# L0's tail: six row additions and six squeeze products on GpSimd, and a new order of the tail's steps

## The chip, the cores and the metric

The kernel runs on one core of one Trainium2 chip. The metric is the time of one execution in microseconds (us). A core has five engines that run their own instruction queues in program order and wait for each other through semaphores: TensorE (PE, matmuls; its weight loads are listed as PEld), VectorE (DVE), ScalarE (ACT), GpSimd (POOL) and SyncE (SP, which here issues most of the DMAs). All data is float32.

## The reference

The reference sends x, 8 batches of 512 tokens with 128 features (32 tiles of 128 tokens), through four layers, L0 to L3. Each layer is half a feed-forward part, an attention part, and half a feed-forward part again:

```
x = x + 0.5 * ffn(LN(x));  x = x + attention(LN(x));  x = x + 0.5 * ffn(LN(x))
```

L0's feed-forward part is a mixture of experts: a router takes the two best of eight experts for each token, with a capacity of 512 rows for each expert. Seven experts are two matrix products with a ReLU between them (128 to 512 to 128), the eighth hands the token through. L1's feed-forward part picks for each token one of 64 small splines by the scores of a cluster and of a tile, compresses the token to two numbers (a product to 32 features, Gelu, a second product to 2 numbers, tanh), evaluates the spline on them, adds the result along a learned direction and normalises again. L1's attention has 16 heads with rotary positions. L2 and L3 follow with other feed-forward and attention parts; the change has nothing to do with them except that some of their weights are made ready inside L0.

## The kernel before

x stays in SBUF for the whole kernel, as one tile of 128 partitions by 4 x 128 elements for each batch. L0 (`l0_block`, lines 493 to 915) runs in stages: the first norms and routing (an order written out by hand in the string FIRST), the first round of experts, MIDDLE (returned rows, attention, second routing), the second round of experts, and then the tail.

**A round of experts** is `experts(wk, ps, n, beside)`. POOL fetches each expert's 512 rows by four indirect DMAs (`fetch`, L664), PE turns them (`turn`, gp L676), PE makes the hidden rows (`inner`, hp L684, with ReLUs on ACT and DVE) and the results (`outer`, op L694), ACT scales them (y L697), and POOL scatters them by four indirect DMAs (`put`, L668) into a DRAM array `yds[n]`. Line order is program order: after each expert's puts a share of the list `beside` is issued. In the first round this list holds `zeros(1)` (four 1 MB DMAs on SP's queue which fill `yds[1]` with zeros from a tile `z`), the handed-through part (`self_part`) of the eight batches, and L1's weights. In the second round it holds the eight `self_part`s, the eight products of L3's adapter weights (`multiply`: pp L1912 on PE, wall L1913 on ACT, then a load of a later pair) and nine steps that add up L2's chosen weights (`adds`). Seven of the eight products are so issued ahead of the last expert's outer product, two of them behind the second expert, and the eighth follows behind the last expert. The round of experts has the PSUM tiles gp/op (tag mm), hp and pp, two buffers for each of the first two tags.

**The tail** is `l0_tail` (lines 919 to 968), called from `l1_block`. Here every engine's order is fixed by the string TAIL, which names steps; for a batch b they are:

- `load` b: two DMAs of 256 KB on SP's queue bring the two sets of returned rows (r, L482); `both` b adds them (L485); `add` b adds the sum to x (L488). For b above 1, `both` is on POOL; `add` is on POOL only if `returned` was called with `aside`, which MIDDLE does and the tail does not.
- `d_sums`, `d_scale`, `d_turn`, `d_keep`: the layer norm of a batch. The first pair of batches is measured on DVE (L248 to L263), the later pairs on POOL (L215 on DVE, L219 to L234 on POOL).
- `squeeze` b in three steps, from `l1_ffn_front`: `_0` the scores (sp L1048, copy L1049), `_1` the first product's bias and Gelu (ht L1054, L1055), `_2` the second product: the multiplication cm (L1060), the reduction cp (L1061) and tanh (comp L1063).
- `ffn0` and `ffn1`: fifteen steps of the spline part (`l1_ffn_steps`, L1087 to L1176) for the batches 0 and 1, with `update0`; `enter` is the norm of L1's attention for batch 0.
- `project0`, `project1`: the projections to q and k with rotary positions (pp L1242, rt L1248, rs L1251); `spread` m g: a permutation by matmuls and its copy (L1263, L1265, L1267); `values`: L1272.
- `turns`: two loads of tables (1 MB and 256 KB); `clear`: memsets on POOL (L1218).

In the order before, `project0` stands in the middle of the string, and the last line is `values ffn1_13 squeeze6_1 clear11 ffn1_14 squeeze7_2 spread02 spread03 spread00 squeeze6_2 spread01`. After the tail L1's attention starts with the scores of batch 0 (s L1290) and the row maxima (nm L1291).

Of the kernel before, what the change touches and what calls it, by code (L numbers as in the profile page):

```python
# [8 lines left out]
F32 = mybir.dt.float32  # L9
I32 = mybir.dt.int32  # L10
AF = mybir.ActivationFunctionType
ALU = mybir.AluOpType
# [46 lines left out]
shares4 c_scale7 whole6 stored7 table7 enter6 shares6 enter7  # L59
"""  # L60
TAIL = """
load1 both1 load0 add1 both0 add0 load3 load6 d_sums0 d_scale0 both3 d_turn0 both6 load2 add3 add6
d_keep0 load4 d_scale1 squeeze0_0 load7 both2 both4 d_turn1 ffn0_0 add2 d_sums2 squeeze0_1 load5 ffn0_1
d_scale3 d_keep1 ffn0_2 d_scale2 turns ffn0_3 add4 ffn0_4 d_turn3 both5 ffn0_5 ffn0_6 both7 d_turn2 add5
squeeze0_2 d_sums4 d_keep2 ffn0_7 squeeze1_0 ffn0_8 squeeze2_0 ffn0_9 d_keep3 ffn1_0 add7 ffn0_10
d_scale4 ffn1_1 ffn1_2 ffn0_11 d_sums6 d_scale5 squeeze2_1 ffn0_12 squeeze1_1 ffn0_13 ffn0_14 ffn1_3
d_scale6 d_turn6 d_scale7 squeeze1_2 d_turn4 d_keep4 d_turn5 squeeze3_0 d_turn7 update0 d_keep5 d_keep6
enter_0 ffn1_4 squeeze4_0 enter_1 squeeze3_1 d_keep7 squeeze5_0 ffn1_5 ffn1_6 clear10 squeeze2_2
squeeze3_2 squeeze5_1 project1 ffn1_7 ffn1_8 spread13 spread12 squeeze4_1 ffn1_9 squeeze5_2 ffn1_10
spread11 spread10 squeeze7_0 clear12 squeeze4_2 project0 ffn1_11 squeeze6_0 ffn1_12 clear02 squeeze7_1  # L70
values ffn1_13 squeeze6_1 clear11 ffn1_14 squeeze7_2 spread02 spread03 spread00 squeeze6_2 spread01
"""

L1F_PLACES = (-63, -58, -58, -55, -50, -50, -48, -47, -42, -42, -39, -37, -34, -31, -26, -22)
# [70 lines left out]
class Net:  # L145
# [316 lines left out]
        return w  # L462

    def zeros(self, n):
        for k in range(4):
            self.nc.sync.dma_start(
                out=self.yds[n][2048 * k : 2048 * k + 2048, :].rearrange("(p n) d -> p (n d)", p=P), in_=self.z)
# [24 lines left out]
    def l0_block(self, w):  # L492
# [8 lines left out]
        with ExitStack() as c:  # L501
# [154 lines left out]
            def experts(wk, ps, n, beside):  # L656
# [23 lines left out]
                def inner(e):  # L680
                    h = hs[e] = wk.tile([P, 4, 512], F32, tag="h", name="h")
                    for ic in range(4):
                        hp = ps.tile([P, 512], F32, tag="hp", name="hp")
                        nc.tensor.matmul(hp, lhsT=w["w1"][:, e, ic * P : (ic + 1) * P], rhs=gts[e], start=True, stop=True)  # L684
                        if ic % 2:
                            nc.vector.tensor_scalar(h[:, ic, :], hp, 0.0, None, ALU.max)
                        else:
                            nc.scalar.activation(h[:, ic, :], hp, AF.Relu)
# [197 lines left out]
                slots(bank)  # L886
            with tc.tile_pool(name="f0w", bufs=2) as wk, tc.tile_pool(name="f0e", bufs=2, space=PSUM) as ps, ordered(engines={*FIXED, mybir.EngineType.SP}):
                more = [lambda: box.__setitem__("w1", self.l1_ffn_weights(self.keep))]
                experts(wk, ps, 0, [lambda: self.zeros(1)] + [lambda b=b: self_part(b) for b in range(NB)] + more)
            with tc.tile_pool(name="f0m", bufs=2) as wk, tc.tile_pool(name="f0c", bufs=7, space=PSUM) as ps, ordered(engines=every):  # L890
                todo, bank = {}, banks(ps)
                load, both, add = self.returned(wk, self.yds[0], 3, True)
# [14 lines left out]
            with tc.tile_pool(name="f0w", bufs=2) as wk, tc.tile_pool(name="f0e", bufs=2, space=PSUM) as ps, ordered(engines=FIXED):  # L907
                w2, more = box["w2"]
                w3, steps = self.l3_ffn_weights(self.keep, wk, ps)
                parts = [lambda b=b: self_part(b) for b in range(NB)]  # L910
                experts(wk, ps, 1, [work for works in zip(parts, steps, more(ps)) for work in works] + [more(ps)[8]])
        return box["w1"], w2, w3

    def apart(self, group, ins):
# [4 lines left out]
    def l0_tail(self, w1, wk, bank, room, clear, turns, enter):  # L919

        todo = {}
        load, both, add = self.returned(wk, self.yds[1], 4)

        def at(name, n, work, *args):
            todo[name] = n, lambda: work(*args)
# [10 lines left out]
        for g in range(4):  # L936
            n = 9 * g
            for k in range(2):
                b = 2 * g + k
                at(f"load{b}", n - 30, load, b)  # L940
                at(f"both{b}", n + 1.3 * k, both, b)
                at(f"add{b}", n + 1.5 + 1.3 * k, add, b)
                scores, *others = self.l1_ffn_front(b, w1, bank, lambda name, shape, k=k: wk.tile([P, *shape], F32, tag=f"{name}{k}", name=name))
                chain(f"squeeze{b}", (n + (16 if b else 14.5) + 1.5 * k, n + 16 + 1.5 * k, n + 19 + 1.5 * k), lambda _, b=b, scores=scores: scores(self.xt[b]), *others)
            self.norms(todo, "d", (2 * g, 2 * g + 1), n + 3.5, bank, quick=not g)
        at("turns", -20, turns)
# [91 lines left out]
    def kept(self, xt):  # L1038
        return xt[:, 0:288].rearrange("p (i c) -> p i c", c=72)

    def l1_ffn_front(self, b, w, bank, room):

        nc = self.nc

# [12 lines left out]

        def finish(ht):
            cm, cp = room("cm", (4, 2, 32)), room("cp", (4, 2))
            nc.vector.tensor_tensor(cm, bc(ht, 2, 2), bc(w["cw2"].rearrange("p (n j) -> p n j", n=2), 1, 4), ALU.mult)  # L1060
            nc.vector.tensor_reduce(cp, cm, AX.X, ALU.add)  # L1061
            for n in range(2):
                nc.scalar.activation(w["comp"][b][:, :, n], cp[:, :, n], AF.Tanh, bias=w["cb2"][:, n : n + 1])  # L1063
# [1026 lines left out]
```

## Time and profile before

| What | us |
| --- | --- |
| Three timed runs | 2604.12, 2608.65, 2613.46 |
| Their median | 2608.65 |
| The profiled execution | 2601.68 |
| Its span in the profile | 2599.8 |
| First experts, fetch to last put (in the span's time) | 59 to 131 |
| Second experts | 259 to 337 |
| Tail, from the first POOL work after the puts to the first s of L1 | 336.6 to 417.0 |

The mean granted TensorE clock of the profiled execution is 0.963. Over the whole span PE is busy 91% of the time, DVE 78%, ACT 68%, POOL 44%. Times in the views are in us from the span's start. A timeline row gives start and duration, engine, line, operation, output and inputs, shapes and, in brackets, the engine's idle time before it with what ended it; the count at the end says how many instructions lie in the row. A window row gives for each engine the busy time in that stretch and the number of instructions, then the granted clock (PEclk), the DMA share and the transfer rate.

### The profile page before, as it was taken

The page shows a single profiled execution, that of the slowest core. Times are in us where ns is not written, and L with a number is a line of the kernel's source. Part 1 is how long each engine was busy: PE and PEld are TensorE (multiplying, and loading weights), DVE is VectorE, ACT ScalarE, POOL GpSimd, SP SyncE. Part 2 cuts the span into 40 slices and gives each one's busy share as a digit, 9 for nine tenths or more (in the row PEclk, how much of TensorE's full clock was granted, in tenths as well). Part 3 has the DMA queues.
Part 4 walks back from the last instruction along what each step waited for, and adds up shares of the span by engine and source line. Part 5 has one row for each costly group of instructions (what it writes and reads, how often), then busy time and mean ns, then how long its engine had stood idle before and what let it go on. Part 6 is the DMA issues. An engine that isn't in the chain of part 4 may idle for free.

```text
span 2599.8 us, 51330 instructions
## 1 busy us (share of the span) xinstructions
PE 2375.4 (91%) x18184; PEld 1421.3 (55%) x18184; DVE 2019.7 (78%) x5582; ACT 1761.3 (68%) x4413; POOL 1154.4 (44%) x2016
## 2 busy tenths in 40 slices
PE   6868938999999998999999999999899999999997
PEld 6546623344444344565555655656565666666664
DVE  5356368888888847878878787876788989898897
ACT  2244233666677666866767667676688998999996
POOL 5754751444454332264352634432234545454443
PEclk9978957999999999999999999999899999999999
DMA  8221330001010100000000000000000000000000
GB/s 272 59 79 42 107 97 1 19 19 27 20 26 19 35 2 4 1 1 1 1 1 1 1 1 1 1 1 17 1 18 15 5 22 22 10 14 22 22 2 13
DMA packets 72976, 66.51 MB, mean 26 GB/s; under 512 B 15690, under 2 KB 62802, under 8 KB 70578
## 3 DMA queue, kind: packets, MB, share of 16 engines
q1 hardware_dynamic: 68112, 54.88, 7.8%
q0 software_dynamic: 3584, 7.58, 1.1%
q8 instruction: 145, 2.38, 0.4%
q10 hardware_dynamic: 1026, 0.78, 0.1%
q14 instruction: 109, 0.89, 0.1%
HBM read 36.47 MB, written 26.80 MB: 24 GB/s over the span
## 4 chain that ended last, share of the span: by engine, by line
PE 63%; DVE 21%; ACT 8%; POOL 4%; issue 2%; DMA 1%; SPq 0%; ACTq 0%; DVEq 0%; POOLq 0%
PE tp L1477 8%; PE s L1451 6%; PE s L1290 5%; PE o L1804 4%; PE o L1493 4%; PE o L1320 4%; PE s L1753 4%; PE yp L384 3%; PE s L1310 3%; ACT e L1760 3%; DVE nm L1291 3%; DVE nm L1455 3%; PE tp L1779 2%; PE pp L1721 2%; PE hp L684 2%
## 5 line engine op out<-in xcount | busy, mean ns | idle before, releaser
L1462 ACT ACTIVATE e<-s,nm 128x512 f32<-128x512 f32 x512 | 345.0, 688 | 25.9 <-DVE nm L1455 21.4
L1291 DVE TENSOR_REDUCE nm<-s 128x2 f32<-128x1024 f32 x256 | 301.3, 1218 | 75.8 <-PE s L1310 60.9
L1455 DVE TENSOR_REDUCE nm<-s 128x2 f32<-128x1024 f32 x256 | 300.9, 1216 | 29.8 <-PE s L1451 27.8
L1483 ACT ACTIVATE p<-tp 128x512 f32<-128x512 f32 x512 | 278.7, 617 | 63.8 <-PE tp L1477 63.8
L1312 ACT ACTIVATE pr<-s 128x512 f32<-128x512 f32 x512 | 271.5, 601 | 73.1 <-PE s L1310 69.5
L1477 PE MATMUL tp<-cst,e 128*128 128x128 f32 x2048 | 292.8, 281 | 15.2 <-DVE rs L1468 7.9
L1477 PEld LDWEIGHTS tp<-cst,e 128*128 128x128 f32 x2048 | 220.1, 141 | 153.7 <-issue 87.4
L1471 POOL TENSOR_SCALAR e<-e,rs 128x512 f32<-128x512 f32 x113 | 198.3, 1755 | 230.0 <-DVE rs L1468 191.5
L1290 PE MATMUL s<-k,q 32*128 32x512 f32 x1024 | 279.4, 658 | 18.0 <-DVE nm L1291 14.7
L1310 PE MATMUL s<-q,k 32*128 32x512 f32 x1024 | 290.3, 627 | 5.4 <-DVE at L1333 4.3
L1760 ACT ACTIVATE e<-e,m 128x512 f32<-128x512 f32 (+3 forms) x512 | 286.3, 571 | 12.7 <-DVE m L1757 12.5
L1757 DVE CUSTOM_DVE_ANT_0 e<-s,bias 128x512 f32<-128x512 f32 (+3 forms) x512 | 220.1, 486 | 93.2 <-PE s L1753 92.7
L219 POOL TENSOR_TENSOR d<-st 128x4 f32<-128x4 f32 (+3 forms) x90 | 19.5, 217 | 549.4 <-DVE st L215 351.3
L1781 ACT COPY pt<-tp 128x512 f32<-128x512 f32 x320 | 174.4, 589 | 90.3 <-PE tp L1779 90.2
L1471 DVE TENSOR_SCALAR e<-e,rs 128x512 f32<-128x512 f32 x399 | 195.6, 520 | 9.1
L1790 DVE TENSOR_SCALAR e<-e,rc 128x512 f32<-128x512 f32 (+3 forms) x512 | 190.0, 416 | 9.1
L386 DVE SCALAR_TENSOR_TENSOR x<-yp,sel,x 128x128 f32<-128x128 f32 x480 | 166.8, 348 | 32.4 <-PE yp L384 20.9
L1779 PE MATMUL tp<-cst,e 128*128 128x128 f32 x1280 | 171.0, 278 | 9.8 <-ACT pt L1781 4.0
L1451 PE MATMUL s<-k,q 32*128 32x512 f32 x1024 | 174.7, 651 | 5.1 <-ACT e L1462 2.6
L1753 PE MATMUL s<-qk 64*128 64x512 f32 (+3 forms) x1024 | 173.4, 457 | 2.0 <-DVE m L1757 1.3
L1493 PE MATMUL o<-p,va 128*32 128x128 f32 x4096 | 165.8, 277 | 2.9 <-ACT p L1483 2.9
L1779 PEld LDWEIGHTS tp<-cst,e 128*128 128x128 f32 x1280 | 139.2, 141 | 48.5 <-issue 13.6
(476 smaller groups left out, 4844.7 us busy)
## 6 DMA issues: line engine op xcount, KB each, us to landing
yd<-z SPq DMA_DIRECT2D x8, 1024.0 KB
r<-yd SPq DMA_DIRECT2D x32, 256.0 KB
sk<-pu SPq DMA_DIRECT2D x16, 256.0 KB
k<-sk SPq DMA_DIRECT2D x60, 64.0 KB
w<-in_l_w SPq DMA_DIRECT2D x14, 256.0 KB
xd<-wqkv SPq DMA_DIRECT2D x12, 256.0 KB
x<-in_x SPq DMA_DIRECT2D x8, 256.0 KB
up<-in_l_up SPq DMA_DIRECT2D x8, 256.0 KB
```

Of the source, the lines that this page charges most:

```text
L1290: nc.tensor.matmul(s[:, jj, :], lhsT=q[cut, g, i * P : (i + 1) * P], rhs=k[cut, g, :], start=True, stop=True)
L1291: nc.vector.tensor_reduce(nms[b, g // 2][:, i, 2 * h : 2 * h + 2, g % 2], s, AX.X, ALU.max, negate=True)
L1310: nc.tensor.matmul(s, lhsT=k[cut, g, kt * P : (kt + 1) * P], rhs=q[cut, g, :], start=True, stop=True)
L1451: nc.tensor.matmul(s[:, jj, :], lhsT=q[cut, g, i * P : (i + 1) * P], rhs=k[cut, g, :], start=True, stop=True)
L1455: nc.vector.tensor_reduce(nm, scores[n, h], AX.X, ALU.max, negate=True)
L1462: nc.scalar.activation(e, s[:, jj, :], AF.Exp, bias=nm[:, jj : jj + 1], accum_out=sm[:, jj : jj + 1])
L1471: (nc.gpsimd if h and jj and 14 <= n < last - 1 else nc.vector).tensor_scalar(e, e, rc[:, jj : jj + 1], None, ALU.mult)
L1477: nc.tensor.transpose(tp[:, kt, :], probs[n][j][:, kt * P : (kt + 1) * P], self.ident)
L1483: nc.scalar.activation(p, turns[n].pop(0), AF.Exp)
L1753: nc.tensor.matmul(s[:, jj, 0:w], lhsT=qs[n][cut, i * P : (i + 1) * P], rhs=ks[n][cut, 0:w], start=True, stop=True)
L1760: outs.append(lambda e=e, jj=jj: nc.scalar.activation(e, e, AF.Exp, bias=mins[n][:, jj, i : i + 1], scale=-1.0, accum_out=sums[n][:, jj, i ...
L1779: nc.tensor.transpose(tp[:, k, :], block(n, jj, i, kt), self.ident)
```

## The change

Six things change.

1. TAIL is a new order of the same steps. `project0` and its four `spread`s now stand at the end, `project1` and `values` earlier; `turns` moves ahead of the loads of the batches 4, 5 and 7; the adds of the batches 2, 3 and 6 follow each other.
2. The tail calls `returned` with `aside`: `add` of the batches 2 to 7 (six instructions) goes from DVE to POOL.
3. `l1_ffn_front` gets an engine for cm: for the batches 2 to 7 (six instructions) the multiplication is on POOL in the tail; the reduction behind it stays on DVE.
4. `zeros(1)` is issued after the third `self_part` instead of ahead of the first, and a small DVE memset of the first column of `z` stands in front, for which its four DMAs wait.
5. hp has three PSUM buffers instead of two, in both rounds.
6. In the second round only the first five products and adds stay beside the experts. The other three products and four adds are issued behind the last expert.

On the engines this moves twelve instructions from DVE to POOL and adds one memset to DVE. Five products instead of seven now stand on PE ahead of the last expert's outer product.

```diff
 TAIL = """
-load1 both1 load0 add1 both0 add0 load3 load6 d_sums0 d_scale0 both3 d_turn0 both6 load2 add3 add6
-d_keep0 load4 d_scale1 squeeze0_0 load7 both2 both4 d_turn1 ffn0_0 add2 d_sums2 squeeze0_1 load5 ffn0_1
-d_scale3 d_keep1 ffn0_2 d_scale2 turns ffn0_3 add4 ffn0_4 d_turn3 both5 ffn0_5 ffn0_6 both7 d_turn2 add5
-squeeze0_2 d_sums4 d_keep2 ffn0_7 squeeze1_0 ffn0_8 squeeze2_0 ffn0_9 d_keep3 ffn1_0 add7 ffn0_10
-d_scale4 ffn1_1 ffn1_2 ffn0_11 d_sums6 d_scale5 squeeze2_1 ffn0_12 squeeze1_1 ffn0_13 ffn0_14 ffn1_3
-d_scale6 d_turn6 d_scale7 squeeze1_2 d_turn4 d_keep4 d_turn5 squeeze3_0 d_turn7 update0 d_keep5 d_keep6
-enter_0 ffn1_4 squeeze4_0 enter_1 squeeze3_1 d_keep7 squeeze5_0 ffn1_5 ffn1_6 clear10 squeeze2_2
-squeeze3_2 squeeze5_1 project1 ffn1_7 ffn1_8 spread13 spread12 squeeze4_1 ffn1_9 squeeze5_2 ffn1_10
-spread11 spread10 squeeze7_0 clear12 squeeze4_2 project0 ffn1_11 squeeze6_0 ffn1_12 clear02 squeeze7_1
-values ffn1_13 squeeze6_1 clear11 ffn1_14 squeeze7_2 spread02 spread03 spread00 squeeze6_2 spread01
+load1 load0 load3 load6 both1 load2 add1 both3 both0 both6 add0 d_sums0 d_scale0 d_turn0 both2 turns
+d_keep0 squeeze0_0 load7 add3 add2 add6 d_sums2 load4 ffn0_0 squeeze0_1 d_scale1 d_turn1 d_scale3 load5
+both4 d_turn3 d_scale2 ffn0_1 add4 ffn0_2 ffn0_3 both5 d_keep1 squeeze0_2 ffn0_4 ffn0_5 d_turn2 ffn0_6
+add5 both7 d_keep2 d_sums4 d_keep3 squeeze1_0 add7 ffn0_7 ffn0_8 ffn1_0 ffn0_9 ffn1_1 d_scale5 ffn0_10
+ffn0_11 d_scale4 d_sums6 d_turn5 d_keep5 squeeze1_1 d_scale7 d_scale6 ffn0_12 clear10 ffn0_13 ffn0_14
+squeeze1_2 ffn1_2 squeeze2_0 d_turn4 squeeze3_0 squeeze5_0 d_turn7 update0 d_turn6 squeeze3_1 d_keep4
+enter_0 ffn1_3 squeeze4_0 clear02 ffn1_4 enter_1 squeeze2_1 squeeze3_2 d_keep7 d_keep6 ffn1_5 ffn1_6
+project1 squeeze5_1 values squeeze4_1 spread13 spread11 clear11 ffn1_7 spread12 ffn1_8 ffn1_9 spread10
+clear12 squeeze2_2 squeeze7_0 ffn1_10 ffn1_11 squeeze5_2 squeeze4_2 ffn1_12 squeeze6_0 ffn1_13
+squeeze6_1 ffn1_14 project0 spread00 spread01 squeeze7_1 spread02 squeeze6_2 spread03 squeeze7_2
 """
...
     def zeros(self, n):
+        if n:
+            self.nc.vector.memset(self.z[:, 0:1], 0.0)
         for k in range(4):
...
-                        hp = ps.tile([P, 512], F32, tag="hp", name="hp")
+                        hp = ps.tile([P, 512], F32, tag="hp", name="hp", bufs=3)
...
-                experts(wk, ps, 0, [lambda: self.zeros(1)] + [lambda b=b: self_part(b) for b in range(NB)] + more)
+                experts(wk, ps, 0, [lambda b=b: self_part(b) for b in range(3)] + [lambda: self.zeros(1)] + [lambda b=b: self_part(b) for b in range(3, NB)] + more)
...
-                experts(wk, ps, 1, [work for works in zip(parts, steps, more(ps)) for work in works] + [more(ps)[8]])
+                adds = more(ps)
+                works = [work for works in zip(parts, steps, adds) for work in works[: 3 if works[1] not in steps[5:] else 1]]
+                experts(wk, ps, 1, works)
+                for work in (*steps[5:], *adds[5:]):
+                    work()
...
-        load, both, add = self.returned(wk, self.yds[1], 4)
+        load, both, add = self.returned(wk, self.yds[1], 4, True)
...
-                scores, *others = self.l1_ffn_front(b, w1, bank, lambda name, shape, k=k: wk.tile([P, *shape], F32, tag=f"{name}{k}", name=name))
+                scores, *others = self.l1_ffn_front(b, w1, bank, lambda name, shape, k=k: wk.tile([P, *shape], F32, tag=f"{name}{k}", name=name), self.nc.gpsimd if b > 1 else None)
...
-    def l1_ffn_front(self, b, w, bank, room):
+    def l1_ffn_front(self, b, w, bank, room, side=None):
...
-            nc.vector.tensor_tensor(cm, bc(ht, 2, 2), bc(w["cw2"].rearrange("p (n j) -> p n j", n=2), 1, 4), ALU.mult)
+            (side or nc.vector).tensor_tensor(cm, bc(ht, 2, 2), bc(w["cw2"].rearrange("p (n j) -> p n j", n=2), 1, 4), ALU.mult)
```

## The prediction

> **What bounds the kernel now.** I read the page's chain first, then a table by stage, then what waits for what in the stages that the change touches. The chain says how small the place is.
>
> ```profile
> PE 63%; DVE 21%; ACT 8%; POOL 4%; issue 2%; DMA 1%; SPq 0%; ACTq 0%; DVEq 0%; POOLq 0%
> ```
>
> Most of the chain is PE work in L1 to L3, which the change leaves alone. It can act only in the two rounds of experts and in the tail, some 230 us of 2600. The table by stage (second experts, then the tail) tells the limit of each.
>
> ```profile
> 259.00:337.00 78.00, 65.22 (x374) 45.91 (x374) 24.95 (x63) 17.78 (x50) 54.50 (x57) 0.92 0.37 104
> 345.00:357.00 12.00, 3.48 (x13) 2.58 (x14) 10.30 (x35) 3.78 (x9) 6.02 (x9) 0.50 0.65 167
> 357.00:377.00 20.00, 8.87 (x32) 6.08 (x32) 18.09 (x59) 12.20 (x29) 11.57 (x25) 0.50 0.23 82
> 377.00:390.00 13.00, 4.84 (x16) 3.33 (x17) 12.05 (x51) 7.38 (x18) 11.28 (x19) 0.50 0.00 0
> 390.00:405.00 15.00, 12.67 (x57) 8.74 (x56) 13.89 (x47) 11.94 (x30) 2.40 (x2) 0.89 0.01 3
> 405.00:417.00 12.00, 8.78 (x41) 5.39 (x40) 11.42 (x36) 3.90 (x12) 3.25 (x13) 1.00 0.00 0
> ```
>
> The third figure group is DVE. In the tail it is busy 10.30 of 12, 18.09 of 20, 12.05 of 13, 13.89 of 15 and 11.42 of 12 us, and the list of its waits in 336 to 417 has only three: 10.0 us for returned rows (9.24 of it ahead of the first `both`) and one of 2.0 us. So the tail is DVE's, and the order of steps can win little idle time, about 2.7 us behind the first addition. In the second experts PE is the busiest, 65 of 78 us. First experts: POOL's 56 indirect DMAs, 0.97 us each with 0.30 us between, stand without a gap from 59.1 to 131; nothing but POOL's queue sets that stage.
>
> In the second round POOL does wait. POOL's timeline, and PE's behind the second expert:
>
> ```profile
> 321.80 0.97 POOL L668 DMA_INDIRECT yd<-y,dst  x1 [2.00 <-ACT y L697]
> 330.34 0.97 POOL L668 DMA_INDIRECT yd<-y,dst  x1 [3.76 <-ACT y L697]
> ```
>
> ```profile
> 284.88 1.06 PE L1912 MATMUL pp<-down,up 128*128 128x128 f32 x8
> 286.44 1.16 PE L1912 MATMUL pp<-down,up 128*128 128x128 f32 x8 [0.50 <-ACT wall L1913]
> 287.43 2.90 PE L684 MATMUL hp<-gt,w 128*128 128x512 f32 x6
> ```
>
> The puts of the last two experts wait for results that PE makes late, and PE spends time on two products in a row, the second behind ACT's copy of the first. That is what parts 5 and 6 touch.
>
> The last view is what a POOL addition does to DVE. DVE's timeline, then POOL's, at the tail's start:
>
> ```profile
> 341.84 0.69 DVE L488 TENSOR_TENSOR x<-x,r 128x512 f32<-128x512 f32 x1
> ...
> 347.10 1.24 DVE L257 TENSOR_TENSOR sm<-st 128x8 f32<-128x8 f32 x1
> ...
> 349.05 1.12 DVE L260 SCALAR_TENSOR_TENSOR h<-h,q 128x8 f32<-128x8 f32 x1
> ...
> 350.60 1.26 DVE L260 SCALAR_TENSOR_TENSOR h<-h,q 128x8 f32<-128x8 f32 x1
> ...
> 352.18 1.89 DVE L488 TENSOR_TENSOR x<-x,r 128x512 f32<-128x512 f32 x3
> ```
>
> ```profile
> 345.28 1.26 POOL L485 TENSOR_TENSOR r<-r 128x512 f32<-128x512 f32 x1 [8.06 <-DMA r<-yd]
> 347.05 1.26 POOL L485 TENSOR_TENSOR r<-r 128x512 f32<-128x512 f32 x1 [0.51 <-DMA r<-yd]
> 348.87 1.27 POOL L485 TENSOR_TENSOR r<-r 128x512 f32<-128x512 f32 x1 [0.56 <-DVE rs L261]
> 350.58 1.26 POOL L485 TENSOR_TENSOR r<-r 128x512 f32<-128x512 f32 x1 [0.43 <-DVE h L259]
> ```
>
> Each of the last three POOL additions has a tiny DVE operation (0.17 us elsewhere in the same chain) that began with it and ended with it: 1.24, 1.12, 1.26. DVE is busy by the record, and does nothing. Beside the first one DVE ran `bn_stats`, which has one input, and lost nothing.
>
> **The change part by part.** All terms go against the profiled execution, 2601.68 us (span 2599.8); the median of the runs, 2608.65, lies 7.0 above it, and I add that at the end.
>
> *DVE's saving.* Three x additions took 1.89 us, 0.63 each; cm takes 0.42 (403.84, 406.08). Six of each: 3.8 + 2.5 = 6.3 us off an engine without idle time.
>
> *What the moved work does to DVE.* The eight two-input POOL operations of this tail stretched DVE by 0 (345.28), 1.07, 0.95, 1.09, 1.85 for two at 361.39, 1.01 (383.03 instead of 0.17) and 0.58 (389.93): 6.55 in all, 0.82 on average for 1.27 of POOL time. Six adds on POOL by that row: 4.9. A 128x256 product on POOL isn't in the trace; its duration lies between 0.56 (the shortest 128x224 POOL operation) and 1.26 (128x512), and I take 0.63, half of the 512, which is the same kind of operation; at the same share it costs 0.41, so 2.5 for six. Together 7.4, with 0 below (all beside one-input work) and 12 x 1.27 = 15.2 above. So the transfer loses about 1 us net where one expects a gain of 6: POOL takes twice as long as DVE for an addition, and DVE stands still for two thirds of that.
>
> The Trainium skill speaks against the change here: "SBUF — State Buffer", section "Who interferes with whom", has VectorE and GpSimd share a port that one of them holds for a whole instruction, which shuts out the other. Taken at its word for every moved operation, the page would give 11.4 us of lock, a tail 5.1 us longer instead of 1.1; the rows agree that a lock exists, and show that it is met only part of the time.
>
> *The order.* Three adds in a row on POOL delay the chain of the first batch (d_sums0 ends at 352.26 now; behind three more additions it ends some 2 us later), and DVE then has less to do until the scores come. `project0` now comes last: behind its rs stand the four permutations (3.59 us on PE at 410.19 for the same work) and a copy of 0.68, where before 7.9 us of other DVE work (408.99 to 416.90) lay beside them. With the squeezes still to do there, DVE has about 2.5 us of copies and 0.8 us of reductions to fill 4.3. I put the exposed end at 1.0 us, between 0 (other work covers it) and 3.6 (nothing does). At half the clock, as PEclk shows it from 336 to 390, 3.6 would come on top; the last two windows granted 0.89 and 1.00, so I leave that out.
>
> *Queues.* SP's now has ten r loads, then rope and perm (1.25 MB, 3.7 us now at 355 to 362), then the last six r loads. These need buffers anyway, four for each tag, and a 256 KB load takes 0.9 us: they land before POOL reaches both4, which is queued behind the adds. The price without that cover is 3.7 us. ACT does two more table loads (1.28 us each now); ACT is busy 12.20 of 20 us at its fullest early window, so they are hidden, up to 2.6 if not.
>
> *Second experts.* Five products instead of seven ahead of the last outer product. The pair behind the second expert takes 2.55 us (284.88 to 287.43), a single one about 1.0: 1.5 saved there, and 1.06 for the other one removed, plus some of the waits: 2.7 us, from 2.0 to 3.5. The three late products run under the puts and the way back of the rows (PE stands idle from 331.5 to 352.8, DVE for 9.24 us), so they cost nothing; without that cover 3.2. A third hp buffer lets PE run ahead of the ReLUs; PE's only wait on DVE there is 0.8 us in total, so 0 to 0.7.
>
> *First experts.* The zeros leave 40 to 57 us and come at about 91, behind a DVE memset of a single column (0.2 us by the smallest DVE rows). They are needed 150 us later. POOL's queue sets the stage, so 0; if slower transfers reach that queue, up to 2.
>
> Sum: -6.3 + 7.4 + 1.0 - 2.7 = -0.6. The profiled execution goes to 2601.1, the median to 2608.1; I say 2608.
>
> **The rivals.** 0.3% of 2608.65, about what a measurement of this kernel can tell from no change, is 7.8 us.
>
> *Locks mostly missed (faster).* If the new order sets the POOL operations beside `bn_stats`, reductions and PSUM copies, as at 345.28, the lock costs nothing, DVE's shorter list sets the tail, and the end is covered: -6.3 - 2.7 = -9.0, 2599.6, from 2596 to 2602. For it: DVE has many one-input operations (24 `bn_stats` L215, 8 cp reductions). Against: MIDDLE, which has its adds on POOL now, shows three POOL additions in a row at 141.57 that stretch L255, L256 and L260 to 1.12, 1.19 and 1.12.
>
> *Locks paid by both (slower).* Each moved operation holds DVE for its whole 1.27 (cm at its upper bound too), and POOL waits as well, as for r at 361.39, 1.71 instead of 1.26, 0.45 for each of six adds on the way to the norms: -6.3 + 15.2 + 2.7 + 1.0 - 2.7 = +9.9, 2618.5, from 2614 to 2623. For it: three of the first four rows above are full. It decides from a cost of (6.3 + 2.7 - 1.0) / 12 = 0.67 us for a moved operation, where my sum has 0.62: the sign of the whole is as close as that.
>
> *It doesn't do what it says.* The moved instructions do stand on POOL; but the zeros and the hp buffers may do nothing. That is inside my sum.
>
> **How the numbers follow.** My sum, 0.40, with its own range of 2602 to 2614, all within 0.3%. Locks missed, 0.33, of which 0.28 lies more than 7.8 below. Locks paid by both, 0.27, of which 0.24 lies more than 7.8 above. So faster 0.28, same 0.48, slower 0.24. The range runs from 2597 to 2620; below and above it about 0.1 each is left out.
>
> **What would show it right or wrong.** In the profile after: DVE's small operations L252 to L263 and L1112 to L1176 beside POOL's L488 and L1060, with their summed stretch over 0.17 to 0.2 (7 us more than now is my sum, none the first rival, 15 the second); the duration of POOL's cm; the POOL wait before the last puts, 3.76 now, and the end of the puts about 2.7 earlier against the first fetch; DVE's idle time between rs of `project0` and the first s; first experts of unchanged length. The forecast is wrong if the tail (336.6 to 417.0, 80.4 us) becomes shorter than 76 or longer than 87, or if L1's loop changes its length though its code does not change.

## The result and the profile after

The changed kernel takes 2614.54 us, the median of 20 runs, against 2608.24 us of the kernel before, measured beside it: ratio 1.0021, 95% interval 1.0012 to 1.0030, or 6.3 us more by the medians (3.1 to 7.8 by the interval). It is inside the range given, but it moved the other way than the forecast of -0.6: almost no gain from the experts, and a tail that is longer by more than the locks.

The profiled execution took 2618.33 us (span 2616.6), 16.7 more than that of before. Only half of this belongs to the change: 8.8 us are there by the 200th row maximum of L1 (826.35 us before, 835.14 after). The other 8.0 come behind it, where some executions of either kernel run more slowly (clock 0.85 at 985 to 1020 us in this profile, 1.00 in that of before): the profile of e1, which has the tail of before, loses 8.1 us there too, and a second one of the changed kernel (e15) 0.9. The tables below therefore use stages up to the first s of L1, which repeat within 1.4 us in nine profiles with the tail of before; the changed tail repeats less well, 86.6 and 84.2 us.

The chain of the kernel after, the same picture:

```profile
PE 63%; DVE 20%; ACT 8%; POOL 4%; issue 2%; DMA 2%; SPq 0%; ACTq 0%; POOLq 0%; DVEq 0%
```

The table by stage of the kernel after (second experts, then the tail in the windows used before, the last one longer). The third figure group is DVE:

```profile
259.00:337.00 78.00, 65.93 (x374) 48.41 (x374) 25.10 (x63) 17.81 (x50) 54.67 (x57) 0.87 0.37 106
345.00:357.00 12.00, 1.29 (x4) 0.68 (x4) 11.24 (x33) 1.65 (x4) 7.69 (x8) 0.50 0.99 297
357.00:377.00 20.00, 9.12 (x29) 5.79 (x29) 15.36 (x40) 11.66 (x26) 14.25 (x25) 0.50 0.01 2
377.00:390.00 13.00, 10.46 (x50) 8.08 (x50) 10.68 (x44) 8.71 (x20) 10.71 (x25) 0.68 0.00 1
390.00:405.00 15.00, 6.44 (x17) 3.97 (x17) 12.04 (x47) 12.23 (x27) 6.23 (x5) 0.57 0.01 2
405.00:417.00 12.00, 9.07 (x44) 6.22 (x43) 9.80 (x31) 6.78 (x17) 3.10 (x3) 0.97 0.00 1
417.00:428.00 11.00, 7.43 (x16) 2.66 (x18) 7.75 (x20) 2.75 (x9) 5.34 (x16) 0.84 0.00 0
```

DVE is busy 15.36 of 20, 10.68 of 13, 12.04 of 15 and 9.80 of 12 us, where it had 18.09, 12.05, 13.89 and 11.42. In the first window it is busier (11.24 instead of 10.30) with fewer instructions: busy by the record, standing still in fact. From the first `both` on DVE to the first s of L1 the tail takes 86.6 us instead of 75.9. DVE still has work of the tail behind the first s, more of it in the old order: to the first row maximum it is 87.8 us instead of 78.8, so 9.0 us of the 10.7 are lost in fact (6.7 in second profiles of both kernels, e9 and e15).

The second experts after: POOL's last puts and the first instruction behind them, then PE's products behind the last expert.

```profile
327.58 0.97 POOL L670 DMA_INDIRECT yd<-y,dst  x1 [1.49 <-ACT y L699]
...
336.83 0.62 POOL L1284 TENSOR_SCALAR bo<-cst,cols 128x128 f32<-128x128 f32 x1 [4.45 <-PE bp L1687]
```

```profile
326.74 1.06 PE L1918 MATMUL pp<-down,up 128*128 128x128 f32 x8
328.30 1.16 PE L1918 MATMUL pp<-down,up 128*128 128x128 f32 x8 [0.51 <-ACT wall L1919]
333.46 2.04 PE L1918 MATMUL pp<-down,up 128*128 128x128 f32 x8 [4.00 <-DMA down<-in_l_down]
335.87 0.79 PE L1687 MATMUL bp<-gb,wb 8*128 8x128 f32 x2 [0.37 <-ACT wall L1919]
```

The wait ahead of the last puts fell from 3.76 to 1.49, and the last put is issued 51.3 us after the round's first put instead of 54.9. But the last product waits 4.00 us for its own load, bp comes behind it, and the tail waits for bp: the loads of the returned rows on SP's queue (2.6 us by the list of waits) and POOL's first operation (4.45). The first `both` runs at 341.01, before at 341.12; from the round's first put that is 60.9 us, before 61.9.

The start of the tail after, DVE and then POOL:

```profile
347.84 1.12 DVE L256 TENSOR_SCALAR rs<-q 128x8 int32<-128x8 int32 x1
...
349.40 1.28 DVE L261 SCALAR_TENSOR_TENSOR rs<-h,rs 128x8 f32<-128x8 f32 x1
350.71 1.18 DVE L259 TENSOR_TENSOR h<-rs 128x8 f32<-128x8 f32 x1
351.93 1.19 DVE L260 SCALAR_TENSOR_TENSOR h<-h,q 128x8 f32<-128x8 f32 x1
353.15 1.18 DVE L261 SCALAR_TENSOR_TENSOR rs<-h,rs 128x8 f32<-128x8 f32 x1
...
354.96 0.17 DVE L263 SCALAR_TENSOR_TENSOR sm<-sm,rs 128x8 f32<-128x8 f32 x1
355.05 1.64 DVE L215 BATCH_NORM_STATS2 st<-x 128x6 f32<-128x128 f32 x8
360.58 0.29 DVE L1060 TENSOR_TENSOR ht<-sp,cb 128x128 f32<-128x128 f32 x1 [3.89 <-ACT xt L1055]
```

```profile
347.66 1.27 POOL L487 TENSOR_TENSOR r<-r 128x512 f32<-128x512 f32 x1 [0.48 <-DMA r<-yd]
349.39 1.26 POOL L487 TENSOR_TENSOR r<-r 128x512 f32<-128x512 f32 x1 [0.46 <-DVE h L260]
350.61 3.70 POOL L490 TENSOR_TENSOR x<-x,r 128x512 f32<-128x512 f32 x3
```

Four small operations in a row now last as long as POOL's four additions. They are the links of the first norm, and DVE then waits 3.89 us for the scores instead of 1.97. That longer wait does not come from the stopped links. The same place in the kernel before:

```profile
352.09 0.17 DVE L263 SCALAR_TENSOR_TENSOR sm<-sm,rs 128x8 f32<-128x8 f32 x1
352.18 1.89 DVE L488 TENSOR_TENSOR x<-x,r 128x512 f32<-128x512 f32 x3
354.10 1.64 DVE L215 BATCH_NORM_STATS2 st<-x 128x6 f32<-128x128 f32 x8
357.71 0.29 DVE L1054 TENSOR_TENSOR ht<-sp,cb 128x128 f32<-128x128 f32 x1 [1.97 <-ACT xt L1049]
```

From the end of the norm (L263) to the scores it is 5.45 us in both kernels. Before, three additions (1.89 us) filled part of that; now they are on POOL, and the wait is longer by about as much. In e5, e8 and e13 it is the same 5.4 to 5.5 us, stopped links or not. DVE's list of waits from 330 to 428 us (bh lies before the tail, and so do 4.0 us of r; the other 1.7 of r were 0.75 before, and the rest summed to 2.0):

```profile
DVE ht L1060 <- ACT xt L1055: 3.9, 1, 3.9
DVE q L1273 <- PE pp L1269: 3.0, 4, 1.3
DVE rt L1254 <- PE pp L1248: 2.3, 2, 1.4
DVE hh L1154 <- PE pa L1144: 2.0, 2, 1.1
DVE st L215 <- POOL x L490: 0.5, 1, 0.5
DVE e L1093 <- ACT e L1087: 0.2, 1, 0.2
```

Without r that is 11.9 us of named waits in place of 2.0.

### The profile page after: what moved, and what is told of

Same layout as the page of the kernel before. It is cut to its first block, busy times and chain, and to the rows that moved or that the text cites. A ratio compares the mean times of both kernels' runs of the same rounds, so it can differ in the third digit from the quotient of the medians.

```text
span 2616.6 us, 51334 instructions
## 1 busy us (share of the span) xinstructions
PE 2387.6 (91%) x18184; PEld 1426.6 (55%) x18184; DVE 2021.9 (77%) x5571; ACT 1765.4 (67%) x4415; POOL 1170.1 (45%) x2028
## 4 chain that ended last, share of the span: by engine, by line
PE 63%; DVE 20%; ACT 8%; POOL 4%; issue 2%; DMA 2%; SPq 0%; ACTq 0%; POOLq 0%; DVEq 0%
PE tp L1483 8%; PE s L1457 6%; PE s L1296 5%; PE o L1810 4%; PE o L1499 4%; PE o L1326 4%; PE s L1759 4%; PE s L1316 3%; PE yp L384 3%; ACT e L1766 3%; DVE nm L1461 3%; DVE nm L1297 3%; PE pp L1727 3%; PE tp L1785 2%; DVE e L1763 2%
## 5 line engine op out<-in xcount | busy, mean ns | idle before, releaser
L1489 ACT ACTIVATE p<-tp 128x512 f32<-128x512 f32 x512 | 279.0, 618 | 62.8 <-PE tp L1483 62.8
L1483 PE MATMUL tp<-cst,e 128*128 128x128 f32 x2048 | 292.8, 281 | 15.2 <-DVE rs L1474 7.9
L1766 ACT ACTIVATE e<-e,m 128x512 f32<-128x512 f32 (+3 forms) x512 | 286.1, 570 | 14.8 <-DVE m L1763 14.6
```

The costliest lines, as they stand in the source:

```text
L1483: nc.tensor.transpose(tp[:, kt, :], probs[n][j][:, kt * P : (kt + 1) * P], self.ident)
L1489: nc.scalar.activation(p, turns[n].pop(0), AF.Exp)
L1766: outs.append(lambda e=e, jj=jj: nc.scalar.activation(e, e, AF.Exp, bias=mins[n][:, jj, i : i + 1], scale=-1.0, accum_out=sums[n][:, jj, i ...
```

## The experiments

Theory: the tail has no slack on DVE, but it is a chain as well; POOL's two-input operations stop links of that chain, POOL's queue hands its results over late, and the gain of the experts is held back by one load. Rivals: the new order alone, above all the projection at its end; or something outside the tail.

By the numbers in the record the experiments ran on five chips, which fall into two groups. On the first two (e1 to e4 on one, e16 on the other) the kernel before took 2608.9 and 2610.5 us; on the other three (e5 to e8, e9 to e12, e13 to e15) 2637 to 2640, since there the first round of experts is 14 to 17 us longer and the second 10 to 12. In the second round PE then stands still at places where the profile shows nothing that it waits for (3.7 us ahead of the first product in e9); why is not known. The tail of before is the same length in both groups (75.6 to 76.9 us in nine profiles), so tails are compared across chips, times only with those of the kernel before on the same chip.

In the table, "own" is what DVE's tail instructions take when nothing stops them (each at the lower quartile of its kind over all these profiles), "stretch" what they took beyond that (from 0.05 us an instruction on), "idle" the gaps between them; the three overlap a little, so they do not add up to the tail.

| Kernel | Ratio to before, 95% interval | Tail | Own | Stretch | Idle |
| --- | --- | --- | --- | --- | --- |
| before; again (e9) | 0.9999, 0.9986 to 1.0012 | 75.9; 76.4 | 70.3 | 8.9; 7.8 | 7.0; 7.5 |
| after | 1.0021, 1.0012 to 1.0030 | 86.6 | 63.7 | 13.5 | 17.7 |
| after again (e15) | 1.0039, 1.0024 to 1.0054 | 84.2 | 63.2 | 12.6 | 16.3 |
| tail's parts 1 to 3 (e2) | 1.0016, 1.0002 to 1.0029 | 86.0 | 63.7 | 12.6 | 18.2 |
| adds and cm, old order (e3) | 1.0019, 1.0008 to 1.0031 | 84.3 | 63.6 | 11.1 | 17.1 |
| adds alone (e5) | 1.0017, 1.0003 to 1.0032 | 79.9 | 66.2 | 13.3 | 9.0 |
| cm alone (e6) | 1.0013, 1.0000 to 1.0027 | 79.6 | 67.7 | 5.9 | 14.0 |
| after, project0 early (e7) | 1.0033, 1.0021 to 1.0045 | 82.4 | 62.8 | 14.6 | 14.0 |
| after, adds as memsets (e8) | 1.0014, 1.0001 to 1.0026 | 79.2 | 63.2 | 6.0 | 17.4 |
| after, adds back on DVE (e13) | 1.0033, 1.0021 to 1.0046 | 82.5 | 67.2 | 7.6 | 15.7 |

**e1 and e2: experts or tail.** e1 is the kernel before with the hunks of zeros, hp and the list beside the second experts; e2 is the kernel before with the other hunks (TAIL, `returned`, `l1_ffn_front`).

```diff
e1: +zeros behind part 3, +bufs=3 for hp, +steps[5:] and adds[5:] behind experts
e2: +new TAIL, +returned(..., 4, True), +cm on nc.gpsimd for b > 1
```

> Parts 4 to 6 alone (zeros later, third hp buffer, three products and four adds behind the experts), the tail as before. My reading of the two traces: the puts end about 3.6 us earlier, but the product moved to the end waits 4 us for its own load, and the loads of the returned rows wait for PE's last small product, so the first both on DVE comes at most 1 us earlier. Theory (gain eaten by the late load): time -1 us, between -2 and 0, tail from the first both to the first s of L1 unchanged at 76 us. Rival (the experts' gain reached the tail, which lost more): -3 us or more.

> Parts 1 to 3 alone (new order, adds and cm on POOL), experts as before. Theory (the loss is the tail's): first both to first s of L1 about 86 us instead of 76, time +7 us (5 to 10), with DVE waiting some 10 us more for ACT, PE and POOL and its small operations stretched by some 13 us instead of 7. Rival (the loss comes from the experts or from the loops behind the tail): under +3.

e1: ratio 0.9981 (0.9970 to 0.9992), 5 us less; first `both` 2.2 us earlier than before, tail 76.9. The gain in time is more than the stage explains, and this was not resolved: the same kernel gave +0.11% on a chip of the second group (e14). e2: tail 86.0, ratio 1.0016, which is 4.2 us, less than the 5 to 10 that I expected. The loss is the tail's. The two ratios together make 0.9997, where the whole change has 1.0021; the difference of 0.24% is a little more than the three intervals leave room for (about 0.19%), and it stays open.

**e9: the kernel before again.** No edit.

> The kernel before, unchanged, for a second profile of it. The stages up to the first s of L1 should repeat within 1 us (tail 75.9); what differs is to show how far L1 and L2 vary by themselves: in the first profile the clock granted at 985 to 1020 us was 1.00, in the changed kernel's 0.85. Expected time: ratio 1.000 within 0.1%.

Ratio 0.9999, tail 76.4, and 31.3 us from the first s to the 65th (before 31.4). With the tail of before, stages up to L1 can be compared to about 1 us; on this chip the experts are longer, which I had not expected.

**e3, e5, e6: which of the moved work.** All in the order of before.

```diff
e5: -self.returned(wk, self.yds[1], 4)
e5: +self.returned(wk, self.yds[1], 4, True)
e6: -l1_ffn_front(b, w1, bank, room)
e6: +l1_ffn_front(b, w1, bank, room, self.nc.gpsimd if b > 1 else None)
e3: both
```

> Parts 2 and 3 alone: the six adds and six cm on POOL with the order of before. If the lock is the loss (6.3 us taken off DVE, but each moved operation stops it for its full length): tail 80 to 84 us instead of 76, time +4 to +8. If the new order is the loss (its waits for PE at the end and for the first norm): tail 76 to 78, time between -1 and +2.

> Part 2 alone: the six adds on POOL, order, cm and experts as before. With both parts on POOL in the old order the tail took 84.3 us instead of 75.9: DVE's own work fell by 6.6, its stretched operations rose by 2.2, and its idle time by 10.1, of which 7.8 stood ahead of cp, waiting for POOL's cm. Theory (the wait for cm in POOL's queue is the loss): adds alone give a tail of 76 to 79 us, time within 2 us of before. Rival (the lock of the adds in the first norm is the loss): 81 us or more, time +4 or more.

> Part 3 alone: the six cm on POOL, order, adds and experts as before. Theory (the reductions behind cm wait on DVE while cm stands in POOL's queue behind norm chains and memsets): 5 to 9 us of DVE waiting for cm, tail 80 to 84 us, time +3 to +7. Rival (lock of the adds): no wait for cm of more than 2 us, tail 74 to 77, time between -2 and +1.

Both parts cost in the old order already: tails of 79.9 with the adds, 79.6 with cm, 84.3 with both, against 76.2. So the order is not the main loss; 8 of the 10 us are there without it (7.4 of 8.2 to the first row maximum, e3 and e2). The two parts lose in different ways. The adds take 4.1 off DVE's own work and add about 5 of stretch and 1 to 2 of idle time. DVE in e5, the first norm again, five links stopped (three beside adds, two beside `both`s that now stand among them):

```profile
379.24 1.19 DVE L259 TENSOR_TENSOR h<-rs 128x8 f32<-128x8 f32 x1
380.46 1.19 DVE L260 SCALAR_TENSOR_TENSOR h<-h,q 128x8 f32<-128x8 f32 x1
381.68 1.18 DVE L261 SCALAR_TENSOR_TENSOR rs<-h,rs 128x8 f32<-128x8 f32 x1
382.90 1.19 DVE L259 TENSOR_TENSOR h<-rs 128x8 f32<-128x8 f32 x1
384.12 1.19 DVE L260 SCALAR_TENSOR_TENSOR h<-h,q 128x8 f32<-128x8 f32 x1
```

The tail of e5, 79.9, is 0.9 above what the theory for it allowed and below the rival's 81: the lock weighs more than I then thought. cm takes 2.6 off DVE's own work, and the six cm on POOL stop DVE for only 0.6 us (L1097 and L1112). The stretch even falls by 2 to 3, by a shift in time: in the kernel before the norm of the second update met an update of x and a memset on POOL (L252, L256 and L257, 2.8 us), and in e6 it meets neither. But the reduction behind cm now waits. The list of waits of e6:

```profile
DVE cp L1061 <- POOL cm L1060: 7.8, 2, 5.1
```

And POOL's timeline in e3, where the same 5.1 us stand in front of the last two cm:

```profile
418.69 0.20 POOL L219 TENSOR_TENSOR d<-st 128x4 f32<-128x4 f32 x1 [2.86 <-DVE st L215]
...
422.99 1.41 POOL L1060 TENSOR_TENSOR cm<-ht,cw 128x256 f32<-128x256 f32 x2
```

The first of the two cm had its input at 417.0, but is queued behind fourteen operations of a norm that wait for DVE and take 4.3 us. In the new order that wait is small (no cp in the list of the kernel after, 0.9 us in e15; its cm comes behind the norm's chain too, but DVE has the copies of q to do).

**e8: lock or occupation.** In the kernel after, each POOL add becomes three memsets of the returned rows' tile; six batches of returned rows are left out of x.

```diff
-            (self.nc.gpsimd if b > 1 and aside else self.nc.vector).tensor_tensor(self.x[b], ...)
+            if b > 1 and bufs == 4:
+                for _ in range(3):
+                    self.nc.gpsimd.memset(got[b, 0], 0.0)
+            else:
+                (self.nc.gpsimd if b > 1 and aside else self.nc.vector).tensor_tensor(self.x[b], ...)
```

> The changed kernel with each of the six POOL adds replaced by three POOL memsets of the same returned-rows tile, which read nothing from SBUF and take POOL about as long (3 x 0.45 us instead of 1.27): the returned rows of six batches are not added to x. Theory (two-input operations of POOL stop DVE's small two-input operations): the four full stops in the first norm (349.4 to 354.3 us) fall to one or none, the stretch in the tail falls from 13.5 to 8 to 10 us, DVE's wait for the first scores from 3.9 to 2 or so, tail 82 to 84 us. Rival (POOL's occupancy, not the lock): stretch and tail within 1 us of the changed kernel's.

Tail 79.2 instead of 86.6 and 84.2, stretch 6.0 instead of 13.5 and 12.6, while POOL is as busy (47.9 us in the tail, 47.3 in the kernel after). DVE and POOL in e8 at the place of the first three adds:

```profile
384.03 0.17 DVE L261 SCALAR_TENSOR_TENSOR rs<-h,rs 128x8 f32<-128x8 f32 x1
384.24 0.17 DVE L259 TENSOR_TENSOR h<-rs 128x8 f32<-128x8 f32 x1
384.44 0.17 DVE L260 SCALAR_TENSOR_TENSOR h<-h,q 128x8 f32<-128x8 f32 x1
384.64 0.17 DVE L261 SCALAR_TENSOR_TENSOR rs<-h,rs 128x8 f32<-128x8 f32 x1
```

```profile
383.71 4.95 POOL L492 MEMSET r<- 128x512 f32 x9
```

The same links run at 0.17 us beside 4.95 us of memsets. So it is what POOL runs that stops these links, its additions and not its memsets, and not POOL being busy; this is shown. The wait for the first scores did not fall (3.89), against my expectation: the links are no longer stopped, but the three additions that used to fill the wait are still not on DVE. By time e8 is at 1.0014, no more than the experts' parts alone in that group (1.0011, e14).

**e13: the adds back on DVE.** e8 also took the adds off DVE, so this is the fair form.

```diff
-        load, both, add = self.returned(wk, self.yds[1], 4, True)
+        load, both, add = self.returned(wk, self.yds[1], 4)
```

> The changed kernel with the six adds back on DVE: new order, cm on POOL and parts 4 to 6 stay. With memsets in their place the tail was 79.2 us; DVE's own work rises by some 4 us when it does the adds itself. Theory (POOL's adds cost DVE more in stopped operations than the 3.8 us they save): tail 81 to 84 us instead of 86.6, the stretch 7 to 9 instead of 13.5, first stop-free norm, time 3 to 5 us under the changed kernel's. Rival (the new order itself, its exposed end and waits, makes the loss, and memsets only freed the norm from waiting for its rows): tail 86 or more.

> The changed kernel, unchanged, for a second profile. If the tail is what is lost, its 86.6 us repeat within 1 us whatever the rest does, and the time is +4 to +8 us against before.

Tail 82.5 beside 84.2 of the changed kernel on the same chip (86.6 in the first profile, so the changed tail repeats within 2.4 us and not the 1 us expected), stretch 7.6 instead of 12.6, own work up by 4.1, and the wait for the first scores back at 2.1. A new wait of 2.7 us comes in, of an add on DVE for POOL's `both`. The adds on POOL cost this order 2 to 4 us of tail, and the ratios (1.0033 and 1.0039) do not separate the two kernels. What stays, some 6 us over before with 15.7 of idle, is that wait, cm and the order: e6, cm in the old order, has 79.6, so the new order adds about 3 here; with both parts on POOL it adds 0 to 2.3 (84.2 and 86.6 against 84.3). The new order without any POOL work was not tried.

**e7: project0 early.** The kernel after, with `project0` and its four `spread`s further forward in the string.

```diff
-... squeeze4_2 ffn1_12 ... ffn1_13 squeeze6_1 ffn1_14 project0 spread00 spread01 ...
+... squeeze4_2 project0 ffn1_12 ... ffn1_13 spread00 squeeze6_1 spread01 ffn1_14 spread02 spread03 ...
```

> The changed kernel with project0 moved forward to behind squeeze4_2, and its four spreads to behind ffn1_13, squeeze6_1 and ffn1_14, as in the order of before; all else as changed. Theory (the projection at the end leaves PE's permutations and DVE's copies without cover): the waits of the copies for PE (3.0 us) and of rt for PE (2.3) mostly go, tail 82 to 84 us instead of 86.6, time 2 to 4 us under the changed kernel's. Rival (the tail is lost earlier, in the first norm and in the waits on ffn1's chain): tail within 1 us of 86.6.

The first s comes 82.4 us after the first `both`, and the waits for q are gone; but the first row maximum comes 6.6 us after that s, since the squeezes now stand behind and cp waits 5.3 us for cm. To the 33rd row maximum it is 151.5 us from the first `both`, in the kernel after 152.9 and 150.7 (e15). So moving `project0` forward exchanges one wait for another and wins nothing; the theory's tail came, its gain did not.

**e4, e10, e12: the experts' parts one by one.**

```diff
e10: +bufs=3 for hp
e12: +zeros behind part 3, behind the memset of one column
e4:  +steps[5:] and adds[5:] behind experts, inputs with bufs=4, load(e + 4) instead of load(e + 2)
```

> Part 6 alone, with four buffers instead of two for the product's inputs, so that the last product's load is issued four products ahead and not behind the third but last. Theory (the late load eats the gain): now no wait on PE for down, the first both comes 2 to 3.5 us earlier than before, time -3 us (-2 to -4). Rival (the way back of the rows or something else on SP's queue sets the first both anyway): under 1 us earlier, time within 1 us.

> Part 5 alone: a third hp buffer. In the second experts hp took 3.60 us for an expert in the kernel with parts 4 to 6 and 3.86 before, with the same matmuls. Theory (the third buffer is a good part of the 3.6 us by which the puts end earlier): the last put of the second experts 1.5 to 2 us earlier, first both 1.5 to 2 earlier, time -1 to -2. Rival (all of it comes from the products moved behind the experts, as the prediction had it): within 0.5 us.

> Part 4 alone: zeros(1) after the third handed-through part, behind a DVE memset. Theory (the first experts are set by POOL's queue, so the transfers' place does not matter): puts of the first experts end within 0.5 us of before, time ratio 1.000 within 0.1%. Rival (the zeros' traffic slows the gathers on the way): first experts 1 to 3 us shorter, time -1 to -3.

e12: ratio 0.9999 (0.9984 to 1.0014), tail and first `both` as in e9 within 1 us, the first experts as long (83.8 and 83.7 us): the zeros' place does nothing, as predicted. e4: 0.9993 (0.9980 to 1.0007). With four loads ahead PE's first gp comes later (by the list of waits it stands 8.7 us for up), so the round started later by 2.4 us and the puts ended 0.2 us earlier: the rival's size, for another reason. e10: 0.9999 (0.9987 to 1.0011) in the second group, where PE stands still elsewhere and the buffer brings nothing. In the first group the parts can be told apart by the time from the second expert's first hp to the last op: 48.3 us in the kernel before, 45.7 in e4 (products moved, two buffers), 44.2 in e1 and e16 (products moved, three buffers). So the products bring 2.6 us and the buffer 1.5: behind the first expert hp takes 3.60 us with three buffers and mostly 3.86 with two.

**e14, e11, e16: the late load mended.** e14 repeats e1. In e11 and e16 the product's inputs have three buffers and the last pair is loaded at the fifth product; e16 leaves the zeros where they were before.

```diff
-            if e + 2 < 8:
-                load(e + 2)
+            if e + 2 < 7:
+                load(e + 2)
+            if e == 4:
+                load(7)
```

> Parts 4 to 6 alone again, beside the kernel before and the two others of this call. Theory (the third hp buffer and the two products fewer shorten the second experts by 3.6 us, of which 1 to 2 reach the tail): time -1 to -3. Rival (nothing reaches the end of the kernel; the -0.19% measured first was the share of executions without the slower stretch of L1 and L2): within 1 us.

> Parts 4 to 6 with the tail as before, and a third buffer for the products' inputs, so that the last pair is loaded with the pair before it, at the fifth product. Theory (the last product's load keeps the gain of the experts from the tail): no wait of PE for down at the end, bp 4 us earlier, the first both 3 to 3.6 us earlier than before instead of 1 to 2.2, time -4 to -6. Rival (loads taken ahead slow the gathers, as four buffers did, where the second experts began 2.4 us later): first both within 1 us of the kernel with parts 4 to 6.

> Parts 5 and 6 without part 4, the tail as before, and the last product's load taken with the one before it. Theory (on a chip where PE does not wait for its instructions in the experts, these parts gain 3 us, and here the wait of 2.5 us for the late load between the last put and the first both is gone): last put to first both 7.0 us instead of 9.5, time -3 to -5 where the second experts take 51 us, within 2 us where they take 65. Rival (parts 5 and 6 bring nothing to the end of the kernel in either case): within 1 us in both.

e14: 1.0011 (1.0002 to 1.0020), e11: 1.0015 (1.0003 to 1.0028), both in the second group, where the second round takes 64.4 to 65.7 us with or without these parts: no gain to pass on. The mended load did its work there too (from the last put to the first `both` 7.0 us in e11, 9.6 in e14), but the time did not follow: both kernels are slower than before (1.6 and 2.8 us by the medians), against theory and rival, and the record does not show why. e16, in the first group: 0.9980 (0.9967 to 0.9992), 5.1 us less than the kernel before on the same chip. PE and POOL of e16:

```profile
329.95 1.16 PE L1918 MATMUL pp<-down,up 128*128 128x128 f32 x8 [0.37 <-ACT wall L1919]
331.48 0.48 PE L1685 MATMUL bp<-gb,wb 8*128 8x128 f32 x2 [0.37 <-ACT wall L1919]
```

```profile
331.51 0.96 POOL L668 DMA_INDIRECT yd<-y,dst  x1 [0.30 <-ACT wall L1919]
333.95 0.61 POOL L1282 TENSOR_SCALAR bo<-cst,cols 128x128 f32<-128x128 f32 x1 [1.47 <-DMA yd<-y,dst]
```

bp is done at 332 instead of 337, POOL waits for its own puts as it did before (1.47), and the first `both` runs at 338.35, 2.8 us earlier than before (3.6 against the round's first put): from the last put 6.8 us, before 7.0, in e1 8.4, after 9.6. That the late load held the experts' gain back is shown, by e16 against e1 and by e11 against e14. The time gained is somewhat more than the 2.8 us by which the first `both` is earlier; its interval (2.1 to 8.6 us) contains that.

## Why the prediction was wrong

The sum was -6.3 + 7.4 + 1.0 - 2.7. By terms:

- **DVE's saving, -6.3.** Right as work: DVE's own work fell by 6.6 us (70.3 to 63.7). But 1.9 us of it, three additions, had filled a wait for the scores and came back as idle time.
- **Stopped operations, +7.4.** Too high: the stretch rose by 4.6 us (8.9 to 13.5), or 4.8 from e9 to e15. For the adds 0.82 an operation was right, 4.9 in the sum and 4.4 to 5.5 in e5. For cm I had counted 2.5 more; it stopped DVE for 0.6 us in e6 and 0.9 in the kernel after, and the rest of the stretch shifted besides. cm's duration was 0.72 us where I had taken 0.63.
- **The order, +1.0.** This is the step that failed. It stood for all new idle time of DVE, and that rose by 10.7 us (7.0 to 17.7). I had looked for it at the end alone. There the copies of q do wait (3.0 us in the first profile, 1.4 in e15), but without these waits others take their place (e7). The rest lies where DVE has lost the work that filled its waits, or waits for what was moved: 1.9 us more for the first scores, 0.9 more for the second batch's returned rows, 2.3 for the projection to q and k (rt), 2.0 for the spline's product (hh), and in the old order 7.8 for cm (e6). I had seen the first of them ("DVE then has less to do until the scores come") and did not price it, and I named nobody who waits for cm, though the step has a reduction on DVE right behind it. How much of these waits the new order would show without any work on POOL stays open.
- **Second experts, -2.7.** The puts do end 3.6 us earlier. The products bring what I had counted (2.6), the third hp buffer 1.5, which I had at 0 to 0.7. But "so they cost nothing" was wrong for the three late products: the cover of 21 us was there, yet the last one's load waits for a buffer until the first of the three has run, and the tail waits for bp behind it. This term failed too: of the 2.7 only 1.0 reached the first `both`. The price that I gave for a missing cover, 3.2, was paid nearly in full: the time from the last put to the first `both` grew from 7.0 to 9.6 us.
- **First experts, 0, and the rope loads, 0.** Right (e12; ends of the first puts within 1 us).

The sum by the measured terms, -6.6 + 4.6 + 10.7 - 1.0 (the last one the first `both` against the first put of the round), is +7.7, near the 6.3 measured; terms that overlap make more of that uncertain than the difference. By the prediction's own measure, from the first POOL work behind the puts to the first s, the tail went from 80.4 to 90.8 us, past the 87 that it had named as its limit. The rival "locks paid by both" had the right sign and +9.9, but by luck: its lock is 15.2 us where 4.6 came, and it did not contain the waits on DVE. The point from which it decides, 0.67 us for a moved operation, left out that work given to another engine must come back in time.

On the Trainium skill's page "SBUF — State Buffer", section "Who interferes with whom": the runs agree that one engine is shut out for the other's whole instruction (1.18 to 1.28 us for operations of 0.17), and that an instruction which reads nothing from SBUF does not do it to two-input operations (e8). Taken at its word for every moved operation, the prediction's estimate of the lock was 11.4 us; 4.6 to 4.8 came.

## What to carry to other kernels

An engine without idle time is not yet a sum of its work: ask of each moved operation which wait it filled, who reads its result, and what stands ahead of it in the queue it is moved into. A helper that stops the full engine can give back all that it takes off (the adds: 4.1 us off, 4.4 to 5.5 of stretch), and gives it back inside the dependent chain of tiny operations, where each link can be stopped for a whole large one. When work is deferred under a gap, follow its loads and what waits for the last of it, not only the engine that runs it; one more buffer for the late load turned a gain at the tail's start of 2.2 us (e1; 1.0 in the kernel after) into 3.6 (e16), against the round's first put.

## What the runs showed of the hardware that was not expected

- Small DVE operations with two SBUF inputs (0.17 us) took 1.18 to 1.28 us while POOL ran a 128x512 addition (1.26), and ran at 0.17 beside POOL memsets of the same length. An integer TENSOR_SCALAR with one input was stopped too, by an addition (1.12 at 347.84 in the kernel after, beside r at 347.66) and also by a memset (1.32 at 387.03, beside a memset of 1.80 at 386.52); the two-input operation behind it ended with that memset as well, and whether it was stopped itself or only waited behind the first is not shown.
- A multiplication of 128x256 with broadcast inputs takes POOL 0.72 to 0.76 us (once 1.12), DVE 0.42.
- A third PSUM buffer for hp shortened the same eight matmuls from 3.86 to 3.60 us an expert in the first group of chips, and brought nothing to the time in the second (e10), where the rounds of experts took 10 to 17 us longer.
